# Two attention layers on one core: weight loads on a second queue, four MLP pieces moved behind the last attention, and one group-norm product a step later

## The chip, the cores and the metric

The kernel runs on one core of a Trainium2 chip. A core has a matrix engine (TensorE, PE in the profile; PEld is its weight load), a vector engine (VectorE, DVE), a scalar engine (ScalarE, ACT), GpSimd (POOL) and a queue for transfers (SyncE, SP). They run side by side, each with its instructions in a fixed order, and wait for each other by semaphores. Transfers are issued from the queues of SP, ACT and POOL. The metric is the device time of one execution in microseconds (us), median of three runs.

## The reference

The input x is 16 images of 256 channels and 32 x 32 positions, so S = 1024 tokens of C = 256 channels, all in float32. Two layers follow each other:

```
# layer 0: 4 heads of 64
qkv = xs @ w_proj + b_proj
x   = softmax(q k^T * 64**-0.5) v @ w_out + b_out + xs
# layer 1: 8 heads of 32
x   = x + attention(group_norm(x))          # qkv_w, proj_w, proj_b, phys_bias
h   = group_norm(x)                         # 32 groups of 8 channels
x   = x + w2 @ gelu(w1 @ h + b1) + b2       # 1024 hidden channels
```

The group norms take mean and variance over 8 channels and all positions of an image, so all tokens of a layer's attention have to be there before the next matrix product can begin.

## The kernel before, in words

Channels (or keys) lie on the 128 partitions, tokens along the free dimension. An image stays in SBUF in two channel halves (CC = 2) of 1024 tokens; a matrix product takes 512 tokens at a time (NT = 2). Every float32 product is two instructions in the trace.

An attention (`attention`, line 248) goes over four items: two token blocks times two channel halves. For each of the eight key blocks of an item it makes scores (`s_a` in layer 0, `s_b` in layer 1, line 262), exponentials on ACT (line 274), and one step later the weighted values (`acc_a`, `acc_b`, line 283); DVE adds the exponentials up (line 300). A step is three key blocks in layer 0 (11 steps) and one in layer 1 (32 steps). When an item is complete, ACT copies the sum out, and two steps later `normalise` (line 306) multiplies the summed exponentials with ones (`den_a`, `den_b`, line 310); ACT reads that twice (lines 319 and 322), DVE takes the reciprocal (line 325) and multiplies (line 326). Three steps after the second channel half, `project` multiplies with the output weights (`o` or `j`, in `out_proj`), and DVE adds bias and residual (line 357) and takes the norm's statistics (line 361).

After the second token block `group_norm` (line 364) begins. It has three parts: `means` on DVE; `variances`, which multiplies the channel means with a matrix that averages groups (`gm`, line 378); and `apply`, which does the same for the variances (`gv`, line 392), takes the power -0.5 on GpSimd and writes the normalised image (line 405: `xn` after the first norm, `hn` after the second). The names end in `_g` for the first norm of an image and `_h` for the second.

The order of the work is written out by hand. `Later` (line 30) is a list of functions that are due after so many steps; `run` (line 570) takes one step of an attention, calls `later.tick()`, and then calls a filling piece if one has that step's number. `run_pieces` calls pieces one by one with a tick behind each. So the second norm of image b, whose attention has ended, is worked off in the first steps of the next image's layer 0, while the last image's is worked off by `later.flush()` with nothing beside it.

The filling pieces of layer 1's attention of image b are the eight output pieces of the MLP of image b - 1 (`reduce`, line 540: 128 output channels times 256 tokens, eight products deep, and an eviction by DVE at line 552) and the six pieces of layer 0's projection of image b + 1. The first image has none, and the last has the eight outputs alone. The MLP's hidden products (`m<-hn,w`, line 527) run between the two layers. Inside an attention `product` (line 233) cuts 128 output channels into slices of 32 or 64; outside it takes 128.

PSUM is in two pools: three tiles of two banks for scores, projections and pieces, and two single banks (`bank`, line 211) for `acc`, `den`, `gm` and `gv`.

At the start ACT's queue issues the six pieces of `w_proj` (`wp`, line 91: for keys, queries and values, each in two channel halves of 128 x 4 x 64 values), then `w_out` and the other matrices (line 129). SP's queue issues the images, GpSimd's the small vectors (lines 103 to 114).

Of the kernel before, what the change touches and what calls it, by code (L numbers as in the profile page):

```python
# [53 lines left out]
def kernel(  # L54
# [21 lines left out]
    nc = tc.nc  # L76
    B, C, S = x.shape
# [10 lines left out]
    wp = const.tile([P, CC, 3, HEADS0, D0], F32, name="wp")  # L88
    for t in (1, 0, 2):
        for cc in range(CC):  # L90
            nc.scalar.dma_start(
                wp[:, cc, t],
                w_proj[cc * P : (cc + 1) * P, :].rearrange(
                    "p (h t d) -> p t h d", t=3, d=D0
                )[:, t],
            )
# [15 lines left out]
    def load_vec(v, n, name):  # L112
        t = const.tile([P, n], F32, name=name)
        nc.gpsimd.dma_start(t, v.rearrange("(c p) -> p c", p=P))
        return t

    bo = load_vec(b_out, CC, "bo")
    g1w = load_vec(gn1_w, CC, "g1w")
    g1b = load_vec(gn1_b, CC, "g1b")
    g2w = load_vec(gn2_w, CC, "g2w")  # L120
    g2b = load_vec(gn2_b, CC, "g2b")
# [45 lines left out]
    with ExitStack() as first:  # L167
# [4 lines left out]
                g2b=g2b, pjb=pjb, m1b=m1b, m2b=m2b, wo=wo, wq=wq, wpj=wpj, w1=w1,  # L172
# [6 lines left out]
    with tc.If(good == 0):  # L179
        with ExitStack() as again:  # L180
# [4 lines left out]
                    g2b=g2b, pjb=pjb, m1b=m1b, m2b=m2b, wo=wo, wq=wq, wpj=wpj, w1=w1,  # L185
# [5 lines left out]
def first_pass(ctx, tc, x, out, k):  # L191
    nc = tc.nc
    B, C, S = x.shape
    CC, SB, NT = C // P, S // P, S // TB
    HC = k["w1"].shape[2] // P
    later = Later()
# [11 lines left out]
    def wide(name):  # L208
        return ps_s.tile([P, 2, TB], F32, tag="s", name=name)

    def bank(name):
        return ps_a.tile([P, TB], F32, tag="acc", name=name)
# [9 lines left out]
    def load_x(b):  # L222
        t = act.tile([P, CC, S], F32, tag="x", name=f"x_{b}", bufs=3)
        for cc in range(CC):
            nc.sync.dma_start(t[:, cc, :], x[b, cc * P : (cc + 1) * P, :])
        return t
# [6 lines left out]
    def product(o, w, r, **flags):  # L233
        for c0 in range(0, P, cols[0]):
            sl = slice(c0, c0 + cols[0])
            nc.tensor.matmul(o[sl], w[:, sl], r, **flags)  # L236
# [124 lines left out]
                nc.vector.bn_stats(stats[:, co, t, :], y)  # L361


    def group_norm(key, src, stats, gw, gb, y):
        st = {}

        def means():
            mv = small.tile([P, CC, 2], F32, tag="mv", name=f"mv_{key}")
            for cc in range(CC):
                nc.vector.bn_aggr(mv[:, cc, :], stats[:, cc].rearrange("p t k -> p (t k)"))  # L370
            mean_c = small.tile([P, CC], F32, tag="mean_c", name=f"mean_c_{key}")
            nc.vector.tensor_copy(mean_c, mv[:, :, 0])
            st.update(mv=mv, mean_c=mean_c)
            later.after(1, variances)

        def variances():
            ps = bank(f"gm_{key}")
            product(ps[:, :CC], k["gavg"], st["mean_c"], start=True, stop=True)
            mean = small.tile([P, CC], F32, tag="mean", name=f"mean_{key}")
            nc.vector.tensor_copy(mean, ps[:, :CC])  # L380

            dv = small.tile([P, CC], F32, tag="dv", name=f"dv_{key}")
            nc.vector.tensor_sub(dv, st["mean_c"], mean)
            nc.vector.tensor_mul(dv, dv, dv)
            tv = small.tile([P, CC], F32, tag="tv", name=f"tv_{key}")
            nc.vector.tensor_add(tv, dv, st["mv"][:, :, 1])
            st.update(mean=mean, tv=tv)
            later.after(1, apply)

        def apply():  # L390
            ps = bank(f"gv_{key}")
            product(ps[:, :CC], k["gavg"], st["tv"], start=True, stop=True)
            rstd = small.tile([P, CC], F32, tag="rstd", name=f"rstd_{key}")
            nc.vector.tensor_scalar(rstd, ps[:, :CC], EPS, None, ALU.add)
            nc.gpsimd.tensor_tensor(rstd, rstd, k["mhalf"], ALU.pow)
            a = small.tile([P, CC], F32, tag="ga", name=f"ga_{key}")
            nc.vector.tensor_mul(a, rstd, gw)
            ma = small.tile([P, CC], F32, tag="gma", name=f"gma_{key}")
            nc.vector.tensor_mul(ma, st["mean"], a)
            c = small.tile([P, CC], F32, tag="gc", name=f"gc_{key}")  # L400
            nc.vector.tensor_sub(c, gb, ma)
            for t in range(NT):
                sl = slice(t * TB, (t + 1) * TB)
                for cc in range(CC):
                    nc.vector.tensor_scalar(  # L405
                        y[:, cc, sl], src[:, cc, sl],
                        a[:, cc : cc + 1], c[:, cc : cc + 1], ALU.mult, ALU.add,
                    )

        means()  # L410


# [106 lines left out]
    def mlp(b, xb, hn):  # L519
        gs = {}  # L520

        def hidden(t, hp):
            ps = wide(f"m1_{b}_{t}_{hp}")
            for n in range(2):
                hc = 2 * hp + n
                for cc in range(CC):
                    nc.tensor.matmul(  # L527
                        ps[:, n, :],
                        k["w1"][:, cc, hc * P : (hc + 1) * P],
                        hn[:, cc, t * TB : (t + 1) * TB],  # L530
                        start=(cc == 0),
                        stop=(cc == CC - 1),
                    )
                g = work.tile([P, TB], F32, tag="g", name=f"g_{b}_{t}_{hc}", bufs=16)
                nc.scalar.activation(  # L535
                    g, ps[:, n, :], AF.Gelu, bias=k["m1b"][:, hc : hc + 1]
                )
                gs[t, hc] = g

        def reduce(t, co, half):  # L540
            n = TB // 2
            ps = wide(f"m2_{b}_{t}_{co}_{half}")[:, 0, :n]
            for hc in range(HC):
                product(
                    ps,
                    k["w2"][:, hc, co * P : (co + 1) * P],
                    gs[t, hc][:, half * n : (half + 1) * n],
                    start=(hc == 0),
                    stop=(hc == HC - 1),
                )  # L550
            y = xb[:, co, t * TB + half * n : t * TB + (half + 1) * n]
            nc.vector.scalar_tensor_tensor(  # L552
                y, ps, k["m2b"][:, co : co + 1], y, ALU.add, ALU.add
            )
            if half:
                nc.sync.dma_start(
                    out[b, co * P : (co + 1) * P, t * TB : (t + 1) * TB],
                    xb[:, co, t * TB : (t + 1) * TB],
                )

        return (
            [lambda t=t, hp=hp: hidden(t, hp) for t in range(NT) for hp in range(HC // 2)],
            [
                lambda t=t, co=co, half=half: reduce(t, co, half)
                for t in range(NT) for co in range(CC) for half in range(2)
            ],
        )


    def run(stage, fill=None):  # L570
        for n, _ in enumerate(stage):
            later.tick()
            if fill and n in fill:
                fill[n]()

    def run_pieces(pieces):
        for piece in pieces:
            piece()
            later.tick()
# [6 lines left out]
    xs = {0: load_x(0)}  # L586
# [3 lines left out]
    for b in range(B):  # L590
        if b + 1 < B:
            xs[b + 1] = load_x(b + 1)
        xn = act.tile([P, CC, S], F32, tag="res", name=f"xn_{b}")
        run(
            attention_0(
                b, tiles0, xs[b],
                lambda st, b=b, xn=xn: group_norm(
                    f"g{b}", xs[b], st, k["g1w"], k["g1b"], xn
                ),
            )  # L600
        )
        first_qkv = []
        if b + 1 < B:
            tiles0, first_qkv = qkv_0(b + 1, xs[b + 1])
        run_pieces(first_qkv if b == 0 else hidden)
        later.flush()
        fill = outputs + (first_qkv if b > 0 else [])
        last = NT * CC * SB - 1
        tiles1, second_qkv = qkv_1(b, xn)
        run_pieces(second_qkv)  # L610
        hn = act.tile([P, CC, S], F32, tag="gn", name=f"hn_{b}")
        run(
            attention_1(
                b, tiles1, xs[b],
                lambda st, b=b, hn=hn: group_norm(
                    f"h{b}", xs[b], st, k["g2w"], k["g2b"], hn
                ),
            ),
            {n * last // max(len(fill) - 1, 1): piece for n, piece in enumerate(fill)},
        )  # L620
        hidden, outputs = mlp(b, xs[b], hn)
    later.flush()
    run_pieces(hidden + outputs)
# [295 lines left out]
```

## Time and profile before

| | |
|---|---|
| time, median of 3 (range) | 4011.65 us (4010.63 to 4012.56) |
| profiled execution | span 4013.6 us, mean granted TensorE clock 0.997 |
| PE, DVE, ACT, POOL busy | 99%, 62%, 52%, 1% |
| layer 0's attention, images 2 to 15, with the hidden pieces and the second projection | 124.7 us each |
| layer 1's attention, images 2 to 15, with 14 pieces each | 123.2 us each |
| layer 1's attention, first image, no pieces | 80.4 us |
| layer 1's attention, last image, eight pieces | 104.1 us |
| from the last `den_b` to the end | 83.8 us |

The stages are taken from the starts of their first score products in the timeline. In the lines below, a line of the waits reads: who waited, for whom, microseconds in total, how often, longest. A line of the timeline reads: start, duration, engine, source line, operation, what it writes and reads, shape, how many were merged, and in brackets the engine's idle time before it and what ended that. A line of the windows reads: stretch, length, then busy time of PE, PEld, DVE, ACT and POOL with the number of instructions, then the granted clock.

### The profile page before, as it was taken

What the parts mean: (1) busy time and instruction counts of PE and PEld (TensorE: products, weight loads), DVE (VectorE), ACT (ScalarE), POOL (GpSimd) and SP (SyncE); (2) the same over time, 40 slices, a digit from 0 to 9 for tenths busy, and PEclk for the clock granted to TensorE, in tenths of its full rate; (3) what the DMA queues carried; (4) which work ended last, traced back from release to release, by engine and by line L of the source; (5) the groups of instructions that cost most, each with busy time, mean ns of one, the idle gap of its engine ahead of it and who ended that gap; (6) DMA issues with size and microseconds to landing.
All of it is one profiled execution on the core that took longest, in us unless ns stands there. A gap on an engine that the chain in (4) does not pass through costs nothing.

```text
span 4013.6 us, 64073 instructions
## 1 busy us (share of the span) xinstructions
PE 3971.1 (99%) x27957; PEld 1518.4 (38%) x27957; DVE 2481.6 (62%) x2538; ACT 2078.1 (52%) x2623; POOL 32.7 (1%) x54
## 2 busy tenths in 40 slices
PE   9999999999999999999999999999999999999998
PEld 3334343343433434334343343433434334343334
DVE  5684756847467474774747747476574765747563
ACT  4564545545455464554545545465454545646462
POOL 1000000000000000000000000000000000000000
PEclk9999999999999999999999999999999999999999
DMA  2000000000000000000000000000000000000000
GB/s 75 1 1 6 17 1 22 1 9 14 1 22 1 9 14 1 22 1 9 14 3 20 1 14 9 3 20 1 22 1 3 20 1 22 1 6 7 1 9 14
DMA packets 19872, 42.07 MB, mean 10 GB/s; under 512 B 5216, under 2 KB 6752, under 8 KB 19584
## 3 DMA queue, kind: packets, MB, share of 16 engines
q1 hardware_dynamic: 13824, 33.56, 2.3%
q8 instruction: 221, 3.62, 0.4%
q10 hardware_dynamic: 5296, 4.20, 0.4%
q14 instruction: 67, 0.55, 0.0%
q0 software_dynamic: 464, 0.15, 0.0%
HBM read 21.12 MB, written 16.78 MB: 9 GB/s over the span
## 4 chain that ended last, share of the span: by engine, by line
PE 94%; DVE 4%; issue 1%; ACT 0%; DMA 0%; POOL 0%; ACTq 0%; POOLq 0%; DVEq 0%
PE s_b L262 14%; PE acc_b L283 12%; PE m L527 11%; PE m L236 11%; PE s_a L262 11%; PE acc_a L283 11%; PE qk_a L236 6%; PE qk_b L236 6%; PE o L236 3%; PE v_b L236 3%; PE v_a L236 3%; PE j L236 3%; PE den_a L310 1%; PE den_b L310 1%; DVE d_a L325 1%
## 5 line engine op out<-in xcount | busy, mean ns | idle before, releaser
L274 ACT ACTIVATE e_b<-s_b 128x1024 f32<-128x1024 f32 x1024 | 994.0, 1025 | 660.6 <-PE s_b L262 648.1
L300 DVE TENSOR_TENSOR es_b<-es_b,e_b 128x1024 f32<-128x1024 f32 x768 | 888.7, 1216 | 147.8 <-ACT e_b L274 146.2
L262 PE MATMUL s_b<-q,k 32*128 32x512 f32 x4096 | 624.3, 640 | 2.8 <-DVE x L552 1.3
L274 ACT ACTIVATE e_a<-s_a 128x1024 f32<-128x1024 f32 x512 | 488.7, 1024 | 205.3 <-PE s_a L262 174.9
L283 PE MATMUL acc_b<-e_b,v 128*32 128x512 f32 x4096 | 546.1, 604 | 0.0
L262 PE MATMUL s_a<-q,k 64*128 64x512 f32 x2048 | 490.9, 608 | 0.0
L300 DVE TENSOR_TENSOR es_a<-es_a,e_a 128x1024 f32<-128x1024 f32 x384 | 467.2, 1217 | 36.0 <-ACT e_a L274 10.2
L527 PE MATMUL m<-hn,w 128*128 128x512 f32 x1024 | 476.1, 606 | 2.0 <-DVE hn L405 2.0
L283 PE MATMUL acc_a<-e_a,v 128*64 128x512 f32 x2048 | 477.5, 600 | 0.0
L236 PE MATMUL m<-g,w 128*32 128x256 f32 (+1 forms) x7808 | 464.9, 379 | 3.7 <-DVE v L448 3.7
L236 PEld LDWEIGHTS m<-g,w 128*32 128x32 f32 (+1 forms) x7808 | 272.6, 111 | 227.7 <-issue 59.3
L262 PEld LDWEIGHTS s_b<-q,k 32*128 32x128 f32 x4096 | 199.3, 183 | 368.4 <-issue 279.2
L535 ACT ACTIVATE g<-m,m1b 128x512 f32<-128x512 f32 x256 | 170.2, 685 | 315.7 <-PE m L527 315.2
L262 PEld LDWEIGHTS s_a<-q,k 64*128 64x128 f32 x2048 | 181.8, 186 | 282.4 <-issue 241.8
L527 PEld LDWEIGHTS m<-hn,w 128*128 128x128 f32 x1024 | 186.6, 191 | 257.1 <-issue 191.5
L448 DVE TENSOR_TENSOR v<-v_b,eones 128x1024 f32<-128x1024 f32 x32 | 39.2, 1224 | 394.4 <-PE v_b L236 394.4
L300 DVE TENSOR_TENSOR es_b<-e_b,e_b 128x1024 f32<-128x1024 f32 x128 | 151.1, 1222 | 188.6 <-ACT e_b L274 188.6
L325 DVE RECIPROCAL d_a<-d_a 128x512 f32<-128x512 f32 x64 | 214.6, 3353 | 83.1 <-ACT d_a L319 83.1
L283 PEld LDWEIGHTS acc_a<-e_a,v 128*64 128x64 f32 x2048 | 132.8, 136 | 322.2 <-issue 317.6
L236 PE MATMUL qk_a<-x,wp 128*32 128x512 f32 (+1 forms) x1856 | 234.3, 594 | 9.1 <-DMA wp<-in_L_conv_w_proj_dram 9.1
L236 PE MATMUL qk_b<-xn,wq 128*128 128x512 f32 x512 | 226.6, 596 | 3.3 <-DVE xn L405 3.3
L283 PEld LDWEIGHTS acc_b<-e_b,v 128*32 128x32 f32 x4096 | 82.5, 108 | 380.2 <-issue 376.0
(104 smaller groups left out, 2389.5 us busy)
## 6 DMA issues: line engine op xcount, KB each, us to landing
x<-in_x_dram SPq DMA_DIRECT2D x32, 512.0 KB, 4.5
out_dram<-x SPq DMA_DIRECT2D x64, 256.0 KB, 2.0
w<-in_L_conv_mlp_w_dram ACTq DMA_DIRECT2D x2, 1024.0 KB, 11.4
wp<-in_L_conv_w_proj_dram ACTq DMA_DIRECT2D x6, 128.0 KB, 8.5
wq<-in_L_conv_qkv_w_dram ACTq DMA_DIRECT2D x1, 768.0 KB, 8.9
wo<-in_L_conv_w_out_dram ACTq DMA_DIRECT2D x1, 256.0 KB, 5.2
wpj<-in_L_conv_proj_w_dram ACTq DMA_DIRECT2D x1, 256.0 KB, 10.6
bv<-in_L_conv_b_proj_dram POOLq DMA_DIRECT2D x1, 128.0 KB, 7.4
```

Source lines behind the costliest of these rows:

```text
L236: nc.tensor.matmul(o[sl], w[:, sl], r, **flags)
L262: nc.tensor.matmul(tiles[g // 2][:, g % 2, :], kT[g * D : (g + 1) * D, c, kb * P : (kb + 1) * P], qT[g * D : (g + 1) * D, c, t * TB : (t + ...
L274: nc.scalar.activation(e, s, AF.Exp, scale=scale)
L283: nc.tensor.matmul(accs[i][g * D : (g + 1) * D, :], v_of(c * G + g, kb), es[g // 2][:, g % 2, :], start=(kb == 0), stop=(kb == SB - 1),)
L300: nc.vector.tensor_add(d, held[i][n] if kb == 1 else d, e)
L310: nc.tensor.matmul(den[g * D : (g + 1) * D, :], ones_of(c * G + g), sums[i][g // 2][:, g % 2, :], start=True, stop=True,)
L325: nc.vector.reciprocal(d, d)
L448: nc.vector.tensor_tensor(v_dst[:, half * n : (half + 1) * n], ps.rearrange("p a (b h d) -> p (a b) h d", b=2, d=D), b_v.unsqueeze(1).to_b ...
L527: nc.tensor.matmul(ps[:, n, :], k["w1"][:, cc, hc * P : (hc + 1) * P], hn[:, cc, t * TB : (t + 1) * TB], start=(cc == 0), stop=(cc == CC - 1),
L535: nc.scalar.activation(g, ps[:, n, :], AF.Gelu, bias=k["m1b"][:, hc : hc + 1])
```

## The change

It has three parts, each for one place where PE stands still. The first weights: the second channel half of each piece of `wp` is issued by GpSimd in place of ACT, so that two queues issue them. The last image: its layer-1 attention keeps four of the eight filling pieces (now spread over the 32 steps), and the other four run behind the attention, while the last `normalise`, the last projection and the last group norm are due. The second group norm: its first small product (`gm_h`) is due two steps after the means in place of one; the first norm keeps one step.

```diff
     for t in (1, 0, 2):
         for cc in range(CC):
-            nc.scalar.dma_start(
+            (nc.gpsimd if cc else nc.scalar).dma_start(
                 wp[:, cc, t],
...
-    def group_norm(key, src, stats, gw, gb, y):
+    def group_norm(key, src, stats, gw, gb, y, wait):
...
             st.update(mv=mv, mean_c=mean_c)
-            later.after(1, variances)
+            later.after(wait, variances)
...
-                    f"g{b}", xs[b], st, k["g1w"], k["g1b"], xn
+                    f"g{b}", xs[b], st, k["g1w"], k["g1b"], xn, 1
...
         fill = outputs + (first_qkv if b > 0 else [])
+        end = []
+        if b == B - 1:
+            fill, end = fill[:4], fill[4:]
         last = NT * CC * SB - 1
...
-                    f"h{b}", xs[b], st, k["g2w"], k["g2b"], hn
+                    f"h{b}", xs[b], st, k["g2w"], k["g2b"], hn, 2
                 ),
             ),
             {n * last // max(len(fill) - 1, 1): piece for n, piece in enumerate(fill)},
         )
+        run_pieces(end)
         hidden, outputs = mlp(b, xs[b], hn)
```

## The prediction

> **What bounds the kernel now.** I read the page's busy shares and its chain first, then the list of waits of the tensor engine, then the timeline where each wait lies.
>
> ```profile
> PE 3971.1 (99%) x27957; PEld 1518.4 (38%) x27957; DVE 2481.6 (62%) x2538; ACT 2078.1 (52%) x2623; POOL 32.7 (1%) x54
> ...
> PE 94%; DVE 4%; issue 1%; ACT 0%; DMA 0%; POOL 0%; ACTq 0%; POOLq 0%; DVEq 0%
> ```
>
> TensorE (PE) is the bound: 99% busy, 94% of the chain that ended last. The other engines have room, so a microsecond counts only where PE waits, runs at half clock[...]. Its waits, with total, number and longest:
>
> ```profile
> PE qk_a L236 <- DMA wp<-in_L_conv_w_proj_dram: 9.1, 2, 6.4
> PE gm_h L236 <- ACT den_a L322: 4.9, 15, 0.3
> PE j L236 <- DVE ok L630: 3.9, 1, 3.9
> ...
> PE gm_h L236 <- DVE mean_c_h L372: 3.2, 1, 3.2
> PE gv_h L236 <- DVE tv_h L386: 2.2, 9, 0.9
> ```
>
> Three places: the start (weights `wp`), the second group norm (`gm_h`, `gv_h`, once in each of 15 images), and the end (the last out-projection `j`, then the last norm). The change has one part for each.
>
> [...] matmuls of 512 columns step by 0.86 us from 11.13 to about 15.5 and by 0.43 later, and the granted clock reads 0.50 from 3935 to 3940, after a gap of 3.9 us. [...] an issue of `wp` on ACT's queue takes some 0.7 us, and six stand in a row. [...] `bv`, with the same shape as one `wp` piece, took 7.4 us from GpSimd's issue to landing among the other loads, and `bqk` with 0.5 KB took 6.4.
>
> **Part 1, the second group norm's first product a step later.** One image's stretch, PE alone:
>
> ```profile
> 260.54 1.03 PE L310 MATMUL den_a<-es_a,ones 128*64 128x512 f32 x4
> 261.49 1.13 PE L262 MATMUL s_a<-q,k 64*128 64x512 f32 x4
> 262.95 0.28 PE L236 MATMUL gm_h<-mean_c_h,gavg 128*64 128x2 f32 x4 [0.33 <-ACT den_a L322]
> 263.16 1.99 PE L262 MATMUL s_a<-q,k 64*128 64x512 f32 x8
> 265.08 2.79 PE L283 MATMUL acc_a<-e_a,v 128*64 128x512 f32 x12
> 268.03 0.28 PE L236 MATMUL gv_h<-tv_h,gavg 128*64 128x2 f32 x4 [0.15 <-DVE tv_h L386]
> ```
>
> `gm_h` needs a bank of the two-bank pool, and the free one is still being read by ACT's second pass over `den_a`. The wait shown (0.33) is less than the loss[...]. From starts: s to acc with `gm_h` inside is 265.08 − 261.49 = 3.59; the next step without it 271.02 − 268.24 = 2.78: loss 0.81. acc to s with `gv_h` is 268.24 − 265.08 = 3.16; without 273.74 − 271.02 = 2.72: loss 0.44. Together 1.25 per image, the same in all 15.
>
> Built, the changed kernel has `gm_h` behind the three `acc_a` of its step and `gv_h` behind those of the next. What comes without a wait: acc to the next `den_a` starts takes 2.62 (276.52 to 279.14), four small products take 0.21, so acc to s with one inside should be 2.83, 0.11 over 2.72. Two make 0.22; from the other side, both could keep the 0.44 that `gv_h` pays now, 0.88. I take 0.30. Saving 1.25 − 0.30 = 0.95 per image, x15 = 14.2 us (5.5 to 15.5).
>
> Do waits come back? `gm_h` starts at about 266.9; the ACT pass it waits for ends at 262.8. On DVE the mean copy now queues behind the reciprocal (262.33 to 265.68), two adds (1.22 each) and the multiply (0.69), so it runs at about 268.8 and `tv_h` is there at 269.4; `gv_h` comes at 272.5: 3 us of slack. The bank that `gm_h` takes is wanted next by `acc_a` at about 270.8, 2 us after the copy. `hn` moves from 272.4 to about 276.6, while its first reader comes four steps later (5.5 us each). Behind it on DVE stand three adds, then the next reciprocal, at about 280.3 (280.9 now); PE needs that one's result only three steps later.
>
> **Part 2, four MLP pieces kept for the end.**
>
> ```profile
> 3929.78 1.04 PE L310 MATMUL den_b<-es_b,eones 128*32 128x512 f32 x8
> 3930.75 1.13 PE L236 MATMUL j<-res_b,wpj 128*128 128x512 f32 x2
> 3931.61 3.35 DVE L325 RECIPROCAL d_b<-d_b 128x512 f32<-128x512 f32 x1 [1.95 <-ACT d_b L319]
> 3935.02 0.68 DVE L326 TENSOR_TENSOR res_b<-res_b,d_b 128x512 f32<-128x512 f32 x1
> 3935.75 5.49 PE L236 MATMUL j<-res_b,wpj 128*128 128x512 f32 x6 [3.88 <-DVE ok L630]
> 3941.28 1.41 DVE L357 SCALAR_TENSOR_TENSOR x<-j,pjb,x 128x512 f32<-128x512 f32 x2 [4.95 <-PE j L236]
> ```
>
> PE waits for the multiply behind the reciprocal ("ok" only came last by chance), then does `j` at half clock: 11.5 us from `den_b` to DVE's first read of `j`. In the changed order a piece comes ahead of `den_b`, three behind it, then all of `j`. A piece of 16 products at full width takes 3.45 (the end's pieces are 3.45 apart). So 4 x 3.45 = 13.8 + `den_b` 0.97 + `j` at full clock 8 x 0.43 = 3.44 + 0.5 for changes and drain = 18.8: the tail grows by 7.3 us. DVE's reciprocal and multiply (done some 10.2 us after the start) lie beside the pieces, ahead of `j` at 14.8. Behind `j` the norm's chain on DVE and the cold start of the last MLP stay.
>
> What the attention stage gives back is read from the first image, which has no pieces:
>
> ```profile
> 3825.70:3929.80 104.10, 102.57 (x1085) 36.08 (x1087) 83.17 (x75) 66.53 (x79) 0.00 (x0) 1.00 0.03 9
> 149.60:230.00 80.40, 78.16 (x569) 20.12 (x568) 74.90 (x64) 66.34 (x79) 0.00 (x0) 1.00 0.00 1
> ```
>
> (stretch, length, PE, PEld, DVE, ...) Eight pieces cost 104.1 − 80.4 = 23.7, 2.96 each, though one runs 3.57: without them PE waits for DVE (`den_b` and `j` some 3.2 us in sum) and for the first exponentials. With four pieces, at the start, a third, two thirds and the end: the first adds 2.7 and the last 2.2 (differences of the two stages' step starts), the middle two 7.2 less some 2.2 of the stalls: 10 in sum, so about 91 (89.8 if all stalls go, 93.2 if none). Saving 13.0 (10.8 to 14.3), net 13.0 − 7.3 = 5.7 us (3.5 to 7).
>
> **Part 3, first weights by two queues.**
>
> ```profile
> 6.37 2.07 PE L236 MATMUL qk_a<-x,wp 128*128 128x512 f32 x2 [6.37 <-DMA wp<-in_L_conv_w_proj_dram]
> 11.13 5.17 PE L236 MATMUL qk_a<-x,wp 128*128 128x512 f32 x6 [2.69 <-DMA wp<-in_L_conv_w_proj_dram]
> ```
>
> PE's second product reads the third `wp` issue of ACT's queue (key half 0, key half 1, query half 0). In the change query half 0 is second there. ACT's `wo` load, which waits for the second's landing, goes out at 9.45, so that place lands at about 9.4: 1.7 us earlier. The key half that PE needs after it comes by GpSimd: issued at 1.26 + 7.4 as `bv` = 8.7, needed at 9.4 + 1.7. Its bound on the late side is a crowd: `wo` and `wq` (1 MB) now follow at about 3 us instead of 9.5, but stand behind the weights on their queue. The full gain is the whole gap, 2.7; the loss, if the GpSimd path is late, some 1.5. I take 1.7. `pb` now waits for the first GpSimd landing and lands at about 15.5; ACT's first eviction stands behind its exponential, at 16 to 17 instead of 17.2, with three PSUM tiles ahead of it, so PE doesn't notice. Edits of `group_norm`'s argument cost nothing: the first norm keeps 1.
>
> **Sum.** 4011.65 − 14.2 − 5.7 − 1.7 = 3990.0 us.
>
> **Rivals.** (a) Forecast, 3990: chance 0.62. (b) Only the waits as listed are saved: 4.9 + 1.3 at the norm, 3.5 at the end, 1.7 at the start: 11.4, 4000.3. For it: small products may always break the pipeline, as `gv_h` does now; against: its loss of 0.44 goes with a wait. Chance 0.2. (c) Only the norm pays: the first image's stage shows DVE at 93% and takes the pieces' time back[...]: 4011.65 − 14.2 = 3997.5. Chance 0.14. (d) Slower: the DVE work of the norm, 3.5 us with GpSimd's power, now lies just ahead of the next reciprocal, and PE waits 2 us for it in each image: 15 x 2 − 21.6 = +8.4 us, 4020. Against: DVE is 65% busy in this stage (three adds, 3.66 of 5.5 us). Chance 0.04.
>
> **Range and chances.** (a) spans 3985 to 3995 by the bounds above; (b) and (c) reach to 4001. Below 3985 and above 4001 I leave 2 in 10. The bound of 0.2% is 8 us, at 4003.6: (a), (b) and (c) lie under it, 0.92 with their tails; 0.04 within, 0.04 slower.
>
> **What would show it.** Right: no `gm_h` wait on `den_a`; acc to s of 2.8 to 2.9 with each small product inside; each image 0.95 shorter (247.8 to about 246.9); the last attention stage at 91 with `j` starting without a wait at full clock; PE's second start at about 9.4. Wrong: a new wait of PE on DVE in that step, a stage over 94 us, or a start later than 11.13.

## The result and the profile after

The changed kernel takes 3989.8 us, median of 6 runs (3988.8 to 3990.9), against 4012.3 us before, median of 6 (4010.6 to 4014.2): a ratio of 0.9944 (95% interval 0.9931 to 0.9956), or 22.5 us less. The forecast was 3990.0.

The page's busy shares and chain after, for the two lines shown of before:

```profile
PE 3956.8 (99%) x27765; PEld 1522.7 (38%) x27765; DVE 2481.5 (62%) x2538; ACT 2076.9 (52%) x2623; POOL 34.9 (1%) x57
...
PE 97%; DVE 2%; issue 1%; DMA 0%; ACT 0%; POOL 0%; ACTq 0%; POOLq 0%; DVEq 0%
```

The kernel is bound by PE as before, and a little more so: DVE's share of the chain fell from 4% to 2%. PE has 192 instructions fewer, since the four moved pieces are cut into full 128-channel products (16 instructions each in place of 64). PE's waits after:

```profile
PE qk_a L236 <- DMA wp<-in_L_conv_w_proj_dram: 8.6, 2, 6.4
...
PE gm_h L236 <- DVE mean_c_h L372: 3.2, 1, 3.2
PE m L527 <- DVE hn L405: 2.0, 1, 2.0
...
PE gv_h L236 <- DVE tv_h L386: 0.9, 1, 0.9
```

The 15 waits of `gm_h` for `den_a` are gone, those of `gv_h` are down to the last image's, and `j` waits no more. The start went from 9.1 to 8.6 only. The last image's three waits behind `j` stand as they did.

The stages, from the starts of the first score products in the timelines (the profiled executions, 4013.6 and 3987.0 us long):

| stretch | before | after | difference |
|---|---|---|---|
| start to first `s_a` | 33.44 | 33.15 | -0.3 |
| first image's layer 0, up to first `s_b` | 116.19 | 114.49 | -1.7 |
| layer 0, images 2 to 16 | 126.07 + 14 x 124.68 | 124.95 + 14 x 123.56 | -16.8 |
| layer 1, images 1 to 15 | 80.40 + 14 x 123.16 | 80.42 + 14 x 123.18 | +0.3 |
| last layer 1, from `s_b` to `gm_h` | 118.74 | 111.96 | -6.8 |
| `gm_h` to the end | 69.1 | 67.8 | -1.3 |

The sum is -26.6. Two rows are not the change's: -1.7 and -1.3 are stretches behind a gap of PE, in which the clock was halved for longer in one execution than in the other (the granted clock reads 0.50 for 3.4 us before and not at all after in the first, for 10.2 and 6.8 us in the second; last section). The first stretch takes 114.5 us three times, 116.1 to 116.2 nine times and 117.4 once in all the profiled executions, whatever the edit, and `gm_h` to the end takes 67.4 to 69.1 in the four executions that end as the kernel before does. Without the two rows 23.6 remain, near the 22.5 of the medians. The -6.8 is steadier: up to `gm_h` those four executions take 117.5 to 119.1, and the five that end as the changed kernel does 112.0 to 112.2.

One image's norm in the changed kernel, PE alone:

```profile
259.52 2.85 PE L262 MATMUL s_a<-q,k 64*128 64x512 f32 x12
262.29 2.80 PE L283 MATMUL acc_a<-e_a,v 128*64 128x512 f32 x12
264.92 0.23 PE L236 MATMUL gm_h<-mean_c_h,gavg 128*64 128x2 f32 x4
265.08 2.85 PE L262 MATMUL s_a<-q,k 64*128 64x512 f32 x12
267.86 2.79 PE L283 MATMUL acc_a<-e_a,v 128*64 128x512 f32 x12
270.48 0.23 PE L236 MATMUL gv_h<-tv_h,gavg 128*64 128x2 f32 x4
270.65 2.85 PE L262 MATMUL s_a<-q,k 64*128 64x512 f32 x12
```

And two undisturbed steps of the kernel before:

```profile
268.24 2.85 PE L262 MATMUL s_a<-q,k 64*128 64x512 f32 x12
271.02 2.80 PE L283 MATMUL acc_a<-e_a,v 128*64 128x512 f32 x12
273.74 2.85 PE L262 MATMUL s_a<-q,k 64*128 64x512 f32 x12
```

From the start of acc to the start of s it takes 265.08 − 262.29 = 2.79 with `gm_h` inside and 2.79 with `gv_h`, against 273.74 − 271.02 = 2.72 with nothing. The two cost 0.07 each; before they cost 0.81 and 0.44.

The end of the last attention:

```profile
3897.27 3.72 PE L236 MATMUL m<-g,w 128*128 128x256 f32 x16
3900.92 1.07 PE L310 MATMUL den_b<-es_b,eones 128*32 128x512 f32 x8
3901.91 10.63 PE L236 MATMUL m<-g,w 128*128 128x256 f32 x48
3912.38 3.60 PE L236 MATMUL j<-res_b,wpj 128*128 128x512 f32 x8
3919.21 0.35 PE L236 MATMUL gm_h<-mean_c_h,gavg 128*128 128x2 f32 x2 [3.23 <-DVE mean_c_h L372]
```

One piece, `den_b`, three pieces, then `j` in 3.43 us (it steps by 0.43). On DVE the multiply that `j` needs was done at 3907.0, 5.4 us before `j` began: the pieces cover more than the gap.

### The profile page after: what moved, and what is told of

It reads as the page before. It is cut to its first block, busy times and chain, and to the rows that moved or that the text cites. A ratio compares the mean times of both kernels' runs of the same rounds, so it can differ in the third digit from the quotient of the medians.

```text
span 3987.0 us, 63660 instructions
## 1 busy us (share of the span) xinstructions
PE 3956.8 (99%) x27765; PEld 1522.7 (38%) x27765; DVE 2481.5 (62%) x2538; ACT 2076.9 (52%) x2623; POOL 34.9 (1%) x57
## 3 DMA queue, kind: packets, MB, share of 16 engines
q8 instruction: 219, 3.59, 0.4%
## 4 chain that ended last, share of the span: by engine, by line
PE 97%; DVE 2%; issue 1%; DMA 0%; ACT 0%; POOL 0%; ACTq 0%; POOLq 0%; DVEq 0%
PE s_b L262 14%; PE acc_b L283 12%; PE s_a L262 12%; PE acc_a L283 12%; PE m L527 12%; PE m L236 11%; PE qk_a L236 6%; PE qk_b L236 6%; PE o L236 3%; PE v_b L236 3%; PE v_a L236 3%; PE j L236 3%; PE den_a L310 1%; PE den_b L310 1%; DVE es_b L300 1%
```

## The experiments

Every ratio is against the kernel before, timed beside it on the same chip. The median of the kernel before is not the same each time (4012.3 in the result, 4013.5 to 4015.1 here), so two changed versions are compared by what each saves; the intervals are some 5 us to either side for most, so a smaller difference between two versions is read from their traces.

**Each part alone.** First, the norm: the changed kernel without the other two parts.

```diff
-            (nc.gpsimd if cc else nc.scalar).dma_start(
+            nc.scalar.dma_start(
...
-            fill, end = fill[:4], fill[4:]
+            pass
```

> The kernel before with only the second group norm's product a step later. If the loss is what the starts in the timeline show (1.25 us per image, of which the changed kernel keeps 0.13), 15 x 1.12 = 16.8 us go: about 3995.5, and the time from one gm_h to the next falls from 247.8 to 246.7. If only the waits as listed are saved (4.9 + 1.3 us), about 4006.

Measured: 3995.4 us, ratio 0.9953 (0.9939 to 0.9967), 18.1 us less than before (4013.5). Layer 0 of images 2 to 16 is 15 x 1.12 shorter, and each norm looks as in the whole change:

```profile
511.26 2.79 PE L283 MATMUL acc_a<-e_a,v 128*64 128x512 f32 x12
513.88 0.23 PE L236 MATMUL gm_h<-mean_c_h,gavg 128*64 128x2 f32 x4
514.05 2.85 PE L262 MATMUL s_a<-q,k 64*128 64x512 f32 x12
```

The theory of starts holds; the list of waits, which adds to 6.2, showed little over a third of the loss.

Second, the end: one step for both norms and one queue for the weights, four pieces kept.

> The kernel before with only four pieces kept for the end. If the pieces fill the gap behind den_b and spare the half clock of j, 6 to 7 us go: about 4005.5, last attention stage 90 us in place of 104, tail from den_b to DVE's read of j longer by 7.3. If DVE takes the pieces' time back, the stage is 94 or more and the time at 4010 to 4012.

Measured: 4008.9 us, ratio 0.9987 (0.9981 to 0.9994), which is 2.4 to 7.6 us less. From the stage's start to `gm_h` it takes 112.24 in place of 118.74, 6.5 less; the stage up to its end is 90.3. The theory that DVE takes all the time back falls. The medians show 4.6 only; their interval holds the trace's number.

Third, the queues: weights by two queues and nothing else.

> The kernel before with only the first weights by two queues. If the prediction's 1.7 us hold, PE's second start is at 9.4 and the time at 4010.6. If the third queue shares the same engines, as the changed kernel's trace suggests, the second start is at 10.5 to 11 and at most 0.5 us go: not to be told from no change.

Measured: 4014.4 us, ratio 0.9998 (0.9990 to 1.0007): no change that can be told. PE's second start:

```profile
5.99 2.07 PE L236 MATMUL qk_a<-x,wp 128*128 128x512 f32 x2 [5.99 <-DMA wp<-in_L_conv_w_proj_dram]
10.56 15.27 PE L236 MATMUL qk_a<-x,wp 128*128 128x512 f32 x30 [2.51 <-DMA wp<-in_L_conv_w_proj_dram]
```

It is at 10.56, not at 9.4. With one queue and the old order the start scatters: 11.13, 11.94, 10.03 and 13.57 in the kernel before, the two runs above and the last run of this section, and the first score comes at 33.44, 33.71, 31.68 and 35.99. With two queues it is 10.56 to 11.26 and 32.67 to 33.58 in five runs. What the second queue gains is less than this scatter.

**Why the second queue brought so little.** One run takes GpSimd's queue away and keeps the order that PE wants:

```diff
-    for t in (1, 0, 2):
-        for cc in range(CC):
-            (nc.gpsimd if cc else nc.scalar).dma_start(
+    for t, cc in ((1, 0), (0, 0), (1, 1), (0, 1), (2, 0), (2, 1)):
+        if True:
+            nc.scalar.dma_start(
```

> The changed kernel with all six first weights back on ACT's queue, but in the order in which PE wants them: key half 0, query half 0, key half 1, query half 1. If a piece lands by its place in its queue, PE's second start is at 9.4, 1.3 us earlier than in the changed kernel, and the time 3988 to 3989. If it lands by the bytes that all queues have moved, it is at 10.5 or later and the time is that of the changed kernel.

```profile
6.21 2.07 PE L236 MATMUL qk_a<-x,wp 128*128 128x512 f32 x2 [6.21 <-DMA wp<-in_L_conv_w_proj_dram]
9.48 2.07 PE L236 MATMUL qk_a<-x,wp 128*128 128x512 f32 x2 [1.19 <-DMA wp<-in_L_conv_w_proj_dram]
13.58 14.83 PE L236 MATMUL qk_a<-x,wp 128*128 128x512 f32 x28 [2.02 <-DMA wp<-in_L_conv_w_proj_dram]
```

PE's second start, on the query half that is second in the queue, is at 9.48, as the prediction read that place from the kernel before. But then PE waits for the key half until 13.58, the first score is at 35.24, and the time is 3991.7 (ratio 0.9941, 0.9927 to 0.9955), 21.8 us less than before and so no better than the changed kernel. An earlier second start alone was worth nothing here: the last of the pieces decides.

Another run keeps the two queues and moves 2 MB of other bytes behind the weights: the second and third image, the first of which PE needs at 94 us, are issued by GpSimd behind its small vectors.

```diff
-            nc.sync.dma_start(t[:, cc, :], x[b, cc * P : (cc + 1) * P, :])
+            (nc.gpsimd if b in (1, 2) else nc.sync).dma_start(t[:, cc, :], ...)
```

> The changed kernel with the loads of the second and third image (2 MB in the first 24 us) issued by GpSimd behind its small vectors. If these bytes crowd the first weights, PE's second start moves from 10.7 to 8.5 to 9.5 and the time is 1 to 2.5 us shorter, about 3988. If the weights' small packets set their landing, the second start stays at 10.7.

```profile
6.03 16.93 PE L236 MATMUL qk_a<-x,wp 128*128 128x512 f32 x32 [6.03 <-DMA wp<-in_L_conv_w_proj_dram]
22.80 7.07 PE L236 MATMUL v_a<-wp,x 128*128 128x256 f32 x32
29.80 5.42 PE L262 MATMUL s_a<-q,k 64*128 64x512 f32 x24
```

The second wait is gone and the first score comes at 29.80, 3.3 us earlier than in the changed kernel; the time is 3988.0 (0.9935, 0.9921 to 0.9948), 26.1 us less than before. And the same with the weights back on one queue in the old order:

> The changed kernel with late image loads but all first weights on ACT's queue in the old order. If two queues are worth something once the engines are not crowded, the first score starts 1 us or more later than with two queues and late images (29.8). If only the bytes count, it starts at 29.8 plus or minus 0.5.

Measured: PE runs through from 6.12, the first score is at 29.52, the time 3987.4 (0.9931, 0.9917 to 0.9944), 27.7 us less than before. So it is the bytes ahead of the weights, and not the number of queues. The windows agree: in the first 24 us the transfer engines are 97% busy before, 97% in the changed kernel and 99% with late images, at 288, 296 and 295 GB/s. As much moves in all three; with late images the weights come first. In the changed kernel the third image was issued only at 10.7 and 11.5 us, when PE's second piece had landed, so of the two images it is the second that was in that piece's way.

**How many pieces, and where.** Three kept in place of four (`fill[:5], fill[5:]`):

> The changed kernel with three pieces kept for the end in place of four. If the pieces pay only by filling the gap, three are enough (j would start 11.3 us after the stage's end, the multiply it needs is done at about 10.2): the stage grows by some 3.4, the tail shrinks by 3.45, and the time is that of the changed kernel within 0.5 us. If each piece kept is worth a quarter of the part's gain, it is 1.7 us slower.

Measured: 3992.1 us (0.9946, 0.9932 to 0.9960), 22.0 us less than before against 22.5 with four, which the timing can't tell apart; in the trace `gm_h` comes 1.8 us later than with four. `j` starts without a wait, so three do fill the gap, as expected; but the fifth piece in the stage costs 5.3 us there in place of 3.4 (last `acc_b` 94.76 after the stage's start against 89.50). The five pieces lie at steps 0, 7, 15, 23 and 31, and none at the step of `j`, where the changed kernel has one. Behind `j`, PE waits for DVE:

```profile
3866.38 3.62 PE L236 MATMUL j<-res_b,wpj 128*32 128x512 f32 x32
3869.92 1.14 PE L262 MATMUL s_b<-q,k 32*128 32x512 f32 x8
3870.99 1.07 PE L283 MATMUL acc_b<-e_b,v 128*32 128x512 f32 x8
3873.72 1.14 PE L262 MATMUL s_b<-q,k 32*128 32x512 f32 x8 [1.66 <-DVE x L357]
```

In the trace the rival's number came out, for a reason that neither theory had: where the pieces lie in the stage counts, not only how many they are.

All eight kept (`fill, end = [], fill`):

> The changed kernel with all eight pieces kept for the end, so that the last attention has none. If the first image's stage is the model, it takes 80.4 us (90.0 in the changed kernel), with PE's waits for DVE at den_b and j back (some 3.2 us), while the tail grows by 13.8: about 4 us slower than the changed kernel, 3994. If pieces cost the same anywhere, no difference.

Measured: 3986.3 us (0.9932, 0.9918 to 0.9945), 3.5 us faster than the changed kernel as the medians stand (27.8 us less than before against 22.5), where 4 slower was expected. The stage is as expected (last `acc_b` at 79.88, the waits for DVE are back: 1.3 us behind the first `j`, 0.7 at `den_b`), and between `den_b` and `j` there are three pieces as before. The miss lies behind `j`:

```profile
3903.66 3.60 PE L236 MATMUL j<-res_b,wpj 128*128 128x512 f32 x8
3907.09 7.07 PE L236 MATMUL m<-g,w 128*128 128x256 f32 x32
3914.00 0.28 PE L236 MATMUL gm_h<-mean_c_h,gavg 128*128 128x2 f32 x2
3914.14 3.70 PE L236 MATMUL m<-g,w 128*128 128x256 f32 x16
3917.67 0.28 PE L236 MATMUL gv_h<-tv_h,gavg 128*128 128x2 f32 x2
3917.81 3.70 PE L236 MATMUL m<-g,w 128*128 128x256 f32 x16
3921.35 4.88 PE L527 MATMUL m<-hn,w 128*128 128x512 f32 x11
```

Each piece is followed by a tick, and the norm's parts are due after so many ticks, so the last four pieces fall into the norm's own gaps. In the changed kernel these gaps are 6.2 us of waits (3.23, 0.93 and 2.02), and behind them the last MLP begins at half clock (granted 0.50 from 3920.6 to 3927.4): its first 16 products take 9.1 us there and 6.95 here.

From this a version with eight pieces laid by the gaps: three in the attention (at steps 10, 20 and 31, where the changed kernel has its last three), two between `den_b` and `j`, and one each ahead of `gm_h`, `gv_h` and the last MLP, once on the changed kernel and once with the late image loads.

```diff
-            fill, end = fill[:4], fill[4:]
+            fill, end = fill[:3], [None, *fill[3:5], None, *fill[5:]]
...
-            {n * last // max(len(fill) - 1, 1): piece for n, piece in enumerate(fill)},
+            {n * last // max(len(fill) - 1, 1): piece for n, piece in enumerate(fill)}
+            if not end else dict(zip((10, 20, 31), fill)),
```

(`None` is a tick without a piece; the last image's `gm_h` is due one step after the means.)

> The changed kernel with the last image's eight pieces placed by its gaps: three in the attention (steps 10, 20 and 31), two between den_b and j, one each between j, gm_h, gv_h and the last MLP (its gm_h one step after the means again). If pieces pay by filling gaps and keeping the clock, the last MLP starts about 110 us after the stage's start (116.0 in the changed kernel, 113.7 with all eight at the end) and at full clock: 3.7 us below all eight at the end, about 3982.5. If the gain with eight came from emptying the attention, this is slower than it: 3988 to 3990.

> The same with the second and third image's loads behind GpSimd's small vectors. If the start's gain adds (3.3 us earlier first score), about 3979; if the loads come back as waits later, 3982 or more.

Measured: 3984.3 us (0.9923, 0.9909 to 0.9936) and 3981.6 us (0.9916, 0.9903 to 0.9930), 30.8 and 33.5 us less than before. The last MLP starts at 111.25 after the stage's start in both, at full clock (its first 16 products take 6.95 us), against 116.0 in the changed kernel. That is 1.2 us later than expected, and more than that is lost at `den_b`: with no piece ahead of it, it waits 0.64 for DVE's last adds, and then takes 2.11 up to the next piece in place of 0.99:

```profile
3890.82 1.04 PE L283 MATMUL acc_b<-e_b,v 128*32 128x512 f32 x8
3892.51 2.19 PE L310 MATMUL den_b<-es_b,eones 128*32 128x512 f32 x8 [0.64 <-DVE es_b L300]
3894.62 7.17 PE L236 MATMUL m<-g,w 128*128 128x256 f32 x32
```

The second is the fastest of all that ran: 8.2 us below the changed kernel as the medians stand, 7.8 by the profiled executions. That its gain over the first is the start's alone is borne out by the first score (28.99 against 32.87) and by equal stages behind it.

**What `gm_h` waited for.** On the kernel before, ACT's second pass reads the copy in SBUF, which frees the bank of `den_a` earlier.

```diff
-                den, den, AF.Exp, scale=-1.0 / DEN_MIN, accum_out=...
+                sums[i][0][:, 0, :], d, AF.Exp, scale=-1.0 / DEN_MIN, accum_out=...
```

> The kernel before, with ACT's second pass over den reading the copy in SBUF (its result goes to the spent sum of exponentials), so that den's bank is free about 0.6 us earlier, while gm_h stays among the scores. If the bank's wait made the loss, scores to acc with gm_h inside falls from 3.59 to 3.0 to 3.3, but gv_h waits longer since the reciprocal now comes behind that pass. If the place among the scores made it, 3.59 stays. Time 4004 to 4014.

```profile
262.79 1.12 PE L262 MATMUL s_a<-q,k 64*128 64x512 f32 x2
262.91 0.60 ACT L319 ACTIVATE d_a<-den_a 128x512 f32<-128x512 f32 x1 [2.44 <-PE den_a L310]
263.84 0.20 PEld L236 LDWEIGHTS gm_h<-mean_c_h,gavg 128*64 128x64 f32 x4 [0.76 <-ACT d_a L319]
263.85 0.28 PE L236 MATMUL gm_h<-mean_c_h,gavg 128*64 128x2 f32 x4
```

Measured: 4013.7 us, ratio 1.0000 (0.9992 to 1.0009): no change. It does not tell the two causes apart, since more than the bank's release moved. The planner, which saw the bank free sooner, put `gm_h` two score instructions behind `den_a` in place of four, and there it follows ACT's first pass (L319): it starts 2.0 us after `den_a` in place of 2.4, behind the release of the bank in both.

The unchanged total hides two changes. `gv_h` did not wait longer, as was expected, but came to stand behind finished `acc_a` products, where acc to s takes 2.79 as in the changed kernel. In return scores to acc with `gm_h` inside grew from 3.59 to 4.04. The starts show why: in an undisturbed step the twelve score instructions start two at a time, 0.43 to 0.53 us apart; here `gm_h` comes between two of a pair, and four of the twelve start alone, so the scores take eight such starts in place of six. In the kernel before, where the pairs are whole, the starts split the 0.81 into some 0.49 ahead of `gm_h`, where the wait for the bank is (listed as 0.33), 0.21 for its four instructions, and 0.11 more than usual between the first two starts behind it. So its place among the scores would cost about 0.3 without a wait; that is an estimate from these starts, and no run shows it.

## Why the prediction was right

The total came out within 0.2 us, partly by luck: two terms were too small and one too large, which left a saving of 22.5 us where 21.6 was forecast, and the median of the kernel before was 0.7 us higher than the one that the forecast started from.

- **The norm: right, somewhat undersized.** 14.2 forecast, 16.8 in the trace (18.1 by the medians of the part alone). The step that missed is the residue: 0.30 per image was taken between 0.22 and 0.88, and it is 0.13, under the lower bound too. That bound took 0.21 for the four small products, as they take among the scores; behind an `acc` it is 0.16 from their start to the scores' (265.08 − 264.92). The slack on DVE was right: the mean copy ran at 266.4 and `tv_h` was there at 267.2, for a `gv_h` at 270.5. No wait came back in its place, so rivals (b) and (d) fall; the reciprocal behind `hn` began at once when DVE was free, and PE did not wait for it.
- **The end: right.** 5.7 forecast, 6.8 in the trace. The tail from the stage's end to DVE's read of `j` was forecast at 18.8 and took 18.7 (3897.27 to 3916.01). The stage was forecast at 91 and took 90.0, since with a piece at steps 10 and 20 all of PE's longer waits for DVE but one of 0.6 us went. Two of the prediction's sums don't close as written: the terms of the tail add to 18.7, and those of the stage (80.4 and 10) to 90.4, nearer to what came. Rival (c) falls with the second run. That the norm's gaps behind `j` would "stay" was right for this change, and filling them was the next gain.
- **The start: the step failed.** 1.7 forecast; 0.45 at the second start and 0.3 at the first score in the trace, nothing that the medians can tell. The failed step is "that place lands at about 9.4: 1.7 us earlier". On one queue the second place landed at 9.4 to 9.8 us in four executions and at 11.1 in a fifth; with two queues, and the images loaded as early as before, it landed at 10.5 to 11.2 in five. The bytes of the first 9.4 us, in the same executions, show what came between: with two queues GpSimd's moved 0.39 MB in place of 0.06 to 0.11, ACT's only 0.33 to 0.38 in place of 0.45 to 0.51, and the images' still 1.57 in place of 1.59 to 1.70. The prediction feared that the key half by GpSimd would be late, but that landed at 6.95; the query half on ACT's own queue was late. It named the crowd, but looked for it in `wo` and `wq`, and not in the weights' own second queue and the images. It also took one execution's 11.13 as fixed, where the same code gave 10.03 to 13.57. The case that it saw for a second queue was the issue time, some 0.7 us an issue and six in a row; that ACT's and the images' bytes would move more slowly beside GpSimd's, as these numbers show, it left out. The signs named for being right came out, or nearly so, but for this one, and none of those for being wrong did.

## What to carry to other kernels

A small product between large ones can cost far more than its listed wait, here nearly three times as much (16.8 us against 6.2): measure it by the distance of the starts on both sides against a step without it, and put it where its operands and its bank are free. Movable work did best here when it was laid into all the gaps of the last, unaccompanied stage, with a few pieces kept in the stage before, where PE otherwise waits for DVE; where the pieces lay mattered as well as how many there were. With the transfer engines 97% busy, as in the first 24 us here, another queue only changed who came first; keeping back the bytes that were not needed yet brought the first score 3.3 us forward.

## What the runs showed of the hardware that I had not expected

Behind one and the same wait of 3.3 us for `xn` in the first image, PE's clock behaves differently from run to run of the same instructions. Before and after, windows of 2 us from the first product behind it (length, then PE, PEld, DVE, ACT and POOL, then the granted clock):

```profile
127.10:129.10 2.00, 2.00 (x4) 0.98 (x5) 1.30 (x3) 0.00 (x0) 0.00 (x0) 0.85 0.00 0
129.10:131.10 2.00, 2.00 (x4) 0.76 (x3) 0.00 (x0) 0.00 (x0) 0.00 (x0) 0.50 0.00 0
131.10:133.10 2.00, 2.00 (x5) 0.85 (x4) 0.00 (x0) 0.58 (x1) 0.00 (x0) 0.80 0.00 0
```

```profile
126.80:128.80 2.00, 2.00 (x5) 1.04 (x6) 1.31 (x3) 0.00 (x0) 0.00 (x0) 1.00 0.00 0
128.80:130.80 2.00, 2.00 (x6) 0.80 (x6) 0.00 (x0) 0.26 (x1) 0.00 (x0) 1.00 0.00 0
130.80:132.80 2.00, 2.00 (x6) 0.92 (x5) 0.00 (x0) 0.75 (x1) 0.00 (x0) 1.00 0.00 0
```

The first 16 products take 6.97 us at full clock, 8.67 with a slow stretch, and 9.90 once; over the 13 profiled executions 6.97 came three times, 8.57 to 8.67 nine times. In the kernel before the slow stretch does not lie at the gap: in windows of 0.25 us the granted clock reads 1.00 up to 128.25, 0.50 from 128.5 to 131.75 and 1.00 again from 132.0, so it is halved from some 1.4 us after PE has resumed, for about 3.4 us. The length of the gap does not settle it in these traces: the same listed wait of 3.3 us was followed by half clock in ten executions of 13. For an analysis it means that a difference of 1 to 3 us behind a gap of about 3 us need not be an effect of the edit. Filling such gaps, as in the three versions whose pieces fill the norm's gaps at the end, also took this scatter out: there the last MLP's first 16 products took 6.95 us in all three executions.
